# Attention, router and quantized FFN on one core: the out projection's later token tiles by fours with two levels of Strassen-Winograd products, and contexts issued two groups at a time

## The chip, the cores and the metric

The kernel runs on one core of one Trainium2 chip. The metric is the device time of one execution in microseconds (us), median over several runs. TensorE (PE in the profile) multiplies matrices, VectorE (DVE), ScalarE (ACT) and GpSimd (POOL) work element by element, SyncE (SP) issues most of the transfers. Each engine works through its own list of instructions in order; they wait for one another through semaphores.

## The reference, cut to what matters

There are 64 sequences of 64 rows, that is 4096 tokens of 1024 numbers, in float32.

```python
x = x + attn(cond(x))          # cond: einsum('bct,bcd->bdt') with a 64x64 matrix chosen per sequence
                               # attn: qkv = y @ qkvw + qkvb (1024 x 3072); 32 heads of 32; softmax over 64 keys;
                               #       ctx @ attn_ow + attn_ob   (1024 x 1024: "the out projection")
x = x + ffn(cond2(x))          # cond2: x @ W.T + 2 * (top-2 gated low-rank experts)
                               # ffn: int8-like quantized gate, up and down products, silu
```

The change concerns above all `ctx @ attn_ow + attn_ob` and what is added to it, the input x.

## The kernel before, in words

**Tiles.** A token tile is 128 tokens; there are 32, taken as 16 pairs. Attention works on 8 blocks of 4 tiles.

**Strassen-Winograd products.** The large float32 products are not done with 8 products of halves but with 7 (class `Winograd`). The weight matrix is cut into quarters A11 to A22, the tokens' matrix into B11 to B22; sums S1 to S4 of weight quarters and T1 to T4 of token quarters are formed, and `ORDER = (1, 6, 7, 5, 2, 4, 3)` names the seven products, with `A_OF` and `B_OF` their operands. Two products that are to be added share a PSUM bank (`BANK`), so that PE adds the second onto the first: before it may, the engine that has to read the first result alone must have read it. The results are put together by DVE, which adds a PSUM bank to an SBUF tile, and by ACT, which copies.

**Attention** (`attention`). For each block: `conditional` multiplies x by its chosen matrices; `rows_job` makes q and k (each product 4 matmuls of 128x256), `values_job` makes v (8 of 128x256). `run(cost, product, rest)` issues one product on PE and, one product later, its `rest` on DVE and ACT. Beside these run the softmax groups. `group` issues `scores` (two units at once) on PE, then `contexts()`, which issues every waiting group whose transposed probabilities pT are there; softmax, a split of the float32 values into 16-bit planes (`parted`), a DMA transpose (`turned`) and a join (`joined`) follow at planned times, kept in a heap by `at(time, f)`. A group's contexts reach `ctx_d` in DRAM through ACT (`co`). In the first block the weights' sums are made on the chip (`sums`, four operations of DVE or POOL in a row) and stored for the later blocks; in later blocks `chores` halve and combine other weights a piece at a time.

**Out projection** (`OutProjection`). It works by pairs. `pair(p)` gives seven steps of one `product` (4 matmuls of 128x512) and one `rest`. x is loaded from the input and the bias added by POOL (L1140); u1, u2 and u3 are sums of products, added to x by POOL (L1156) or with PSUM by DVE (L1159). `prepare(p + 1)` forms the next pair's T sums on DVE (L1029 to L1032). `turn` splits x into planes and transposes it by DMA, and `turned` joins it and stores it to `xT_d` for the second stage; x itself is stored to the output. Pairs 0 and 1 run inside attention's last phase, beside the last softmax groups; there

```python
length = 24
at(now + 41, contexts)
```

places the last contexts. Pairs 2 to 15 run alone, from `second_stage`, which also loads one 1 MB piece of the next weights W (`loads_t`) per pair.

**Second stage** (`second_stage`). By pairs again: router, seven base products with W, the low-rank part, quantization and the FFN, in an order that is written out by hand. It is not changed but for where its tiles lie and when its weights are loaded.

Matmuls of float32 stand in the records as two instructions each, so a product of 4 matmuls has 8 records.

Of the kernel before, what the change touches and what calls it, by code (L numbers as in the profile page):

```python
# [20 lines left out]
P = 128  # L21
# [15 lines left out]
def adaln_attn_ffn(ctx: ExitStack, tc: tile.TileContext, a, out: bass.AP):  # L37
# [40 lines left out]
    with tc.manual_schedule(), ExitStack() as psum, ExitStack() as early:  # L78
        ps_g = psum.enter_context(tc.tile_pool(name="ps_g", bufs=4, space=PSUM, reuse_waits="tile"))
        st = early.enter_context(tc.tile_pool(name="halve", bufs=2))  # L80
        chores = halve_weights(tc, st, const, dram, srcs, half, any_i)
        chores = itertools.chain(chores, combine_quarters(tc, st, (("wo", a["ow"]), ("wt", a["w_t"])), comb))
        op = OutProjection(tc, a, x_t, out_t, ctx_d, xT_d, ps_g, comb, KC, H)
        attention(tc, a, x_t, ctx_d, ident, dram, ps_g, KC, PB, NBLK, NCH, HPC, H, C, chores, early, op)
        second_stage(tc, a, out_t, xT_d, ident, ps_g, KC, NT, H, C, half, comb, op)

# [96 lines left out]
def attention(tc, a, x_t, ctx_d, ident, dram, ps_g, KC, PB, NBLK, NCH, HPC, H, C, chores, early, op):  # L183
# [27 lines left out]
    with ExitStack() as ctx, ExitStack() as mid:  # L211
# [5 lines left out]
        pTp = pool(ctx, "pT1", 4, side="right")  # L217
        sm = pool(ctx, "sm1", 3, side="right")
        ps_s = pool(ctx, "ps_s", 1, space=PSUM)
# [35 lines left out]

        def held(word, other):


            nc.scalar.copy(word, other[:, 0:1])
# [9 lines left out]
        def sums(eng, at):  # L269
            eng.tensor_tensor(at("S1"), at("A21"), at("A22"), ALU.add)  # L270
            eng.tensor_tensor(at("S2"), at("S1"), at("A11"), ALU.subtract)
            eng.tensor_tensor(at("S3"), at("A11"), at("A21"), ALU.subtract)
            eng.tensor_tensor(at("S4"), at("A12"), at("S2"), ALU.subtract)
# [4 lines left out]
        def load_qk(b, wh, c, eng=None):  # L278
            t = w_qk[b, wh, c] = wp.tile([P, 7, KQ, P], F32, tag="wqk", name=f"w{wh}_{b}_{c}")
            if b == 0:  # L280
# [4 lines left out]
                def rest():  # L285
                    sums(eng or nc.vector, lambda key: t[:, SLOT[key], :, :])
                    nc.gpsimd.dma_start(qk_d[wh, c], t)
                return rest
# [6 lines left out]
        def load_v_raw(g, eng):  # L295
# [9 lines left out]
            def rest():  # L305
                sums(eng, at)
                for slot in range(7):
                    later.append(lambda slot=slot: nc.gpsimd.dma_start(v_d[g][:, slot, :, :], w_v[0, g, slot]))
            return rest

        bqkv = act.tile([P, 3 * KC], F32, tag="bqkv", name="bqkv")
        x_next = load_x(0)
        first_sums = [load_qk(0, "q", 0), load_qk(0, "k", 0, nc.gpsimd)]
        nc.sync.dma_start(bqkv, a["qkvb_t"])
        first_sums.append(load_v_raw(0, nc.gpsimd))
# [62 lines left out]
        def job(name, cost, n, matmuls, put, begin=None, done=None):  # L378
# [4 lines left out]
            def one(i):  # L383
                def product():
                    if i == ORDER[0] and begin:
                        begin()
                    bank = BANK[i]
# [20 lines left out]
            return [one(i) for i in ORDER]  # L408
# [7 lines left out]
        def rows_job(b, c, wh, next_load):  # L416
# [30 lines left out]
            return job(f"ps{wh}{{}}_{b}_{c}", 1.72, HB, matmuls, put, begin, done)  # L447
# [88 lines left out]
        def context(b, c, us, pTs):  # L536
# [11 lines left out]
            for n, u in enumerate(us):  # L548
# [3 lines left out]
                co = p2.tile([P, HB], F32, tag="co", name=f"co_{b}_{c}_{u}")  # L552
                nc.scalar.activation(co, pc[:, n, :], AF.Identity, bias=bqkv[:, 2 * KC + ch:2 * KC + ch + 1])  # L553
                nc.scalar.dma_start(ctx_d[2 * b + t][:, ch, :], co)

# [10 lines left out]
        def contexts():  # L566
            while waiting and len(waiting[0][3]) == 2:
                context(*waiting.pop(0))

        def group(b, c, us):  # L570


            def begin():
                ps = scores(b, c, us)
                contexts()
# [45 lines left out]
        def qk_fill(b, c):  # L621
            fills = []
            for wh in "qk":
                n = qk_jobs.index((b, wh, c))

                def next_load(n=n):
                    if n + 2 < len(qk_jobs):
                        f = load_qk(*qk_jobs[n + 2])
                        if f:
                            pending_sums.append(f)  # L630

                js = rows_job(b, c, wh, next_load)
                if b == 0 and n >= 2:

                    cost, product, rest = js[5]

                    def product_and_sums(product=product):
                        product()
                        if pending_sums:
                            pending_sums.pop(0)()  # L640
                    js[5] = (cost, product_and_sums, rest)
                fills += js
            return fills

        v_raw = []

        def v_fill(b, g):
            def next_load(slot):
                if b == 0 and g + 1 < NV:
                    if slot == SLOT[A_OF[ORDER[-1]]]:  # L650
                        v_raw.append(load_v_raw(g + 1, nc.vector))
# [5 lines left out]
            if (b, g) == (0, 0):  # L657
                cost, product, rest = js[4]

                def product_and_sums():  # L660
                    product()
                    pending_sums.pop(0)()
                js[4] = (cost, product_and_sums, rest)
# [10 lines left out]
        for b in range(NBLK):  # L674
            if b + 1 < NBLK:
                x_next = load_x(b + 1)
            for c in range(NP):
                fills, length = [], None
                if c + 1 < NP:
                    fills += qk_fill(b, c + 1)  # L680
                    if c == 0:
                        fills[7:7] = v_fill(b, 1)
                        if b == 0:
                            cost, product, rest = fills[4]

                            def with_sums(product=product):
                                product()
                                v_raw.pop()()
                            fills[4] = (cost, with_sums, rest)
# [3 lines left out]
                else:  # L693
# [5 lines left out]
                    at(now + 41, contexts)  # L699
# [6 lines left out]
        assert not due and not waiting  # L706
# [350 lines left out]
class OutProjection:  # L1057
# [3 lines left out]
    def __init__(self, tc, a, x_t, out_t, ctx_d, xT_d, ps_g, comb, KC, H):  # L1061
        self.tc, self.a, self.x_t, self.out_t, self.ctx_d, self.ps_g, self.comb = tc, a, x_t, out_t, ctx_d, ps_g, comb
        self.xT_d, self.turning = xT_d, []
        self.KC, self.H = KC, H
        self.NPAIR = len(ctx_d)
        self.stack = ExitStack()
        self.st = {}

    def pool(self, name, bufs):
        return self.stack.enter_context(self.tc.tile_pool(name=name, bufs=bufs, reuse_waits="tile"))  # L1070

    def open_weights(self):

        nc, H = self.tc.nc, self.H
        wp = self.pool("wo3", 1)
        self.cp = [self.pool("co3", 1)]
        ob = self.ob = wp.tile([P, H], F32, tag="ob", name="ob")
        self.A, loads = load_quarters(self.tc, wp, self.comb, "wo", self.a["ow"], self.KC // 2, H // 2)
        return [
            lambda: self.load_ctx(0), loads[0], lambda: nc.sync.dma_start(ob, bcast_rows(self.a["ob"]))  # L1080
        ] + loads[1:]

    def open_rest(self):
        self.cp.append(self.pool("co4", 1))
        self.xp, self.tp, self.up = self.pool("xo3", 2), self.pool("to3", 2), self.pool("uo3", 1)
        self.hp = self.pool("ho3", 2)
# [3 lines left out]
        self.prepare(0)  # L1090

# [5 lines left out]
    def load_x(self, p):  # L1097
        s = self.st.setdefault(p, {})
        s["x"] = self.xp.tile([P, 2, self.H], F32, tag="x", name=f"xo_{p}")
        for t in range(2):  # L1100
            self.tc.nc.sync.dma_start(s["x"][:, t, :], self.x_t[2 * p + t])

    def prepare(self, p):
        s, KQ = self.st[p], self.KC // 2
# [4 lines left out]
    def turn(self, p, t):  # L1109

        nc, n = self.tc.nc, self.H // 2
        for f in range(2):
            h = self.hp.tile([P, 2, n], I16, tag="h", name=f"xh_{p}_{t}_{f}")
            nc.scalar.copy(h, planes(self.st[p]["x"][:, t, f * n:(f + 1) * n]))  # L1114
            hT = self.hp.tile([P, 2, n], I16, tag="hT", name=f"xhT_{p}_{t}_{f}")
            nc.sync.dma_start(
                hT.rearrange("p h (k q) -> p (h k) q", q=P), h.rearrange("p h n -> p (h n)"), transpose=True
            )
# [556 lines left out]
```

## Time and profile before

| what | value |
|---|---|
| median of 3 runs | 2479.53 us (2477.33 to 2479.58) |
| the profiled execution's own time | 2482.55 us |
| its span, first to last instruction | 2480.8 us |
| granted TensorE clock, mean | 0.992 |
| attention, up to the first out projection product | 0 to 1386.6 us |
| out projection, pairs 0 to 15 | 1386.6 to 1784.0 us |
| second stage | 1784.0 to 2480.8 us |
| busy in the out projection alone (1456 to 1788): PE, DVE, ACT, POOL | 332.0, 113.5, 131.9, 120.6 of 332 us |
| DMA there | 0.78 of 16 engines, 241 GB/s |

The page gives busy time by engine, the span in 40 slices, the chain of work that ended last, and the costliest groups of instructions. A row such as `L1159 DVE TENSOR_TENSOR xo<-pod,xo 128x512 ... x29 | 20.0, 690 | 62.6 <-PE pod` says: line 1159, on DVE, 29 times, 20.0 us in all, 690 ns each, and 62.6 us in which DVE stood idle ahead of them, ended by PE. A busy PE is modelled at the ends of its matmuls, so the distance between starts is what one costs.

### The profile page before, as it was taken

The page shows a single profiled execution, that of the slowest core. Times are in us where ns is not written, and L with a number is a line of the kernel's source. Part 1 is how long each engine was busy: PE and PEld are TensorE (multiplying, and loading weights), DVE is VectorE, ACT ScalarE, POOL GpSimd, SP SyncE. Part 2 cuts the span into 40 slices and gives each one's busy share as a digit, 9 for nine tenths or more (in the row PEclk, how much of TensorE's full clock was granted, in tenths as well). Part 3 has the DMA queues.
Part 4 walks back from the last instruction along what each step waited for, and adds up shares of the span by engine and source line. Part 5 has one row for each costly group of instructions (what it writes and reads, how often), then busy time and mean ns, then how long its engine had stood idle before and what let it go on. Part 6 is the DMA issues. An engine that isn't in the chain of part 4 may idle for free.

```text
span 2480.8 us, 34182 instructions
## 1 busy us (share of the span) xinstructions
PE 2435.7 (98%) x13232; PEld 1703.8 (69%) x13232; DVE 1524.9 (61%) x2957; ACT 953.6 (38%) x1303; POOL 360.8 (15%) x451
## 2 busy tenths in 40 slices
PE   8999999999999999999999999999999999999996
PEld 7888888888888888888888644444454545454452
DVE  4585585675764755745646623333367777778787
ACT  1243353443443533533534533343423333333333
POOL 5010011011122221110000233334200000000001
PEclk9999999999999999999999999999999999999997
DMA  8795767676677667766646668877744443434343
GB/s 281 262 266 153 225 192 232 191 208 203 205 201 246 206 188 248 201 202 181 171 145 215 187 213 248 271 232 239 227 151 79 87 79 81 85 73 91 71 96 70
DMA packets 417980, 446.76 MB, mean 180 GB/s; under 512 B 299665, under 2 KB 353938, under 8 KB 404114
## 3 DMA queue, kind: packets, MB, share of 16 engines
q1 hardware_dynamic: 387298, 377.90, 52.5%
q0 software_dynamic: 12080, 49.82, 7.6%
q10 hardware_dynamic: 18432, 16.79, 2.0%
q8 instruction: 106, 1.74, 0.3%
q14 instruction: 64, 0.52, 0.1%
HBM read 272.97 MB, written 100.66 MB: 151 GB/s over the span
## 4 chain that ended last, share of the span: by engine, by line
PE 95%; DVE 3%; DMA 1%; issue 1%; ACT 0%; SPq 0%; ACTq 0%; DVEq 0%
PE pska L428 5%; PE psva L455 5%; PE poc L1019 5%; PE pskc L428 4%; PE psvc L455 4%; PE pskd L428 4%; PE psqd L428 4%; PE pbc L1019 4%; PE pba L1019 4%; PE psvd L455 4%; PE psqa L428 4%; PE poa L1019 4%; PE pod L1019 4%; PE pbd L1019 4%; PE psqc L428 4%; PE s L491 3%
## 5 line engine op out<-in xcount | busy, mean ns | idle before, releaser
L533 ACT COPY pT<-phT 128x1024 int16<-128x1024 int16 x128 | 167.2, 1342 | 84.8 <-DMA phT<-ph 84.6
L553 ACT ACTIVATE co<-c,bqkv 128x256 f32<-128x256 f32 x128 | 60.6, 473 | 295.2 <-PE c L543 253.6
L503 DVE TENSOR_REDUCE mx<-s 128x8 f32<-128x512 f32 x128 | 88.3, 690 | 138.0 <-PE s L491 128.4
L521 ACT COPY ph<-prob 128x1024 int16<-128x1024 int16 x128 | 131.4, 1046 | 43.4 <-DVE prob L515 42.7
L414 DVE SCALAR_TENSOR_TENSOR kbd<-pskd,bqkv,psku 32x256 f32<-32x256 f32 x256 | 122.6, 479 | 30.9 <-PE pskd L428 27.2
L507 ACT ACTIVATE prob<-prob 128x512 f32<-128x512 f32 x128 | 78.9, 628 | 154.4 <-DVE prob L504 130.6
L1140 POOL TENSOR_TENSOR xo<-xo,ob 128x1024 f32<-128x1024 f32 x32 | 82.5, 2597 | 375.7 <-DMA xo<-in_x_dram 371.2
L428 PE MATMUL psqa<-yB,wq 128*128 128x256 f32 x512 | 123.5, 384 | 0.0
L428 PE MATMUL pska<-yB,wk 128*128 128x256 f32 x512 | 122.6, 382 | 0.0
L1483 POOL DMA_DIRECT2D out_dram<-y x29 | 25.2, 869 | 653.4 <-DVE y L1475 653.4
L1114 ACT COPY xh<-xo 128x1024 int16<-128x1024 int16 x64 | 64.1, 1040 | 143.8 <-DVE xo L1159 143.4
L455 PE MATMUL psva<-wv,yB 128*128 128x256 f32 x512 | 117.7, 383 | 0.0
L1019 PE MATMUL poa<-woA,cx 128*128 128x512 f32 x256 | 115.3, 593 | 0.0
L1019 PE MATMUL pba<-wtA,x1T 128*128 128x512 f32 x256 | 115.1, 592 | 0.0
L1125 ACT COPY xTo<-xhT 128x1024 int16<-128x1024 int16 x64 | 84.8, 1341 | 64.1 <-DMA xhT<-xh 62.3
L455 PEld LDWEIGHTS psva<-wv,yB 128*128 128x128 f32 x512 | 96.8, 191 | 13.4
L428 PEld LDWEIGHTS pska<-yB,wk 128*128 128x128 f32 x512 | 96.0, 190 | 14.3 <-issue 1.4
L428 PEld LDWEIGHTS psqa<-yB,wq 128*128 128x128 f32 x512 | 95.2, 190 | 13.7 <-issue 0.2
L513 DVE TENSOR_REDUCE den<-prob 128x8 f32<-128x512 f32 x128 | 86.8, 678 | 17.4 <-ACT prob L507 17.2
L504 DVE TENSOR_TENSOR prob<-s,mx 128x512 f32<-128x512 f32 x128 | 88.6, 692 | 9.7 <-DVE mx L503 0.9
L515 DVE TENSOR_TENSOR prob<-prob,den 128x512 f32<-128x512 f32 x128 | 89.8, 702 | 4.4
L412 ACT ACTIVATE kbd<-pska,bqkv 32x256 f32<-32x256 f32 x128 | 59.6, 466 | 79.2 <-PE pska L428 77.6
(243 smaller groups left out, 5138.5 us busy)
## 6 DMA issues: line engine op xcount, KB each, us to landing
wv<-v_d SPq DMA_DIRECT2D x98, 512.0 KB, 3.8
wq<-q_d SPq DMA_DIRECT2D x28, 1792.0 KB, 8.1
wk<-k_d SPq DMA_DIRECT2D x28, 1792.0 KB, 8.2
x<-in_x_dram SPq DMA_DIRECT2D x32, 512.0 KB, 9.8
ctx_d<-co ACTq DMA_DIRECT2D x128, 128.0 KB, 5.6
cx<-ctx_d SPq DMA_DIRECT2D x16, 1024.0 KB, 7.0
xo<-in_x_dram SPq DMA_DIRECT2D x32, 512.0 KB, 5.7
xT_d<-xTo SPq DMA_DIRECT2D x64, 256.0 KB, 4.1
```

The source lines that it names most:

```text
L414: nc.vector.scalar_tensor_tensor(dst, ps, bias, u, ALU.add, ALU.add)
L428: nc.tensor.matmul(ps[:, 0:HB], A[:, SLOT[A_OF[i]], k, :], B[B_OF[i]][:, k, :], start=first and k == 0, stop=k == KQ - 1, skip_group_check ...
L455: nc.tensor.matmul(ps[:, j * VC:(j + 1) * VC], B[B_OF[i]][:, k, j * P:(j + 1) * P], A[:, k, :], start=first and j == 0 and k == 0, stop=k ...
L503: nc.vector.tensor_reduce(mx_v, ps, AX.X, ALU.max)
L504: nc.vector.tensor_tensor(p.rearrange("p (a e) k -> p a e k", a=2), ps, mx_v.unsqueeze(3).to_broadcast([P, 2, HPC, C]), ALU.subtract)
L513: nc.vector.tensor_reduce(den, p, AX.X, ALU.add)
L515: nc.vector.tensor_tensor(p, p, den.unsqueeze(2).to_broadcast([P, n, C]), ALU.mult)
L521: nc.scalar.copy(h, planes(p.rearrange("p n k -> p (n k)")))
L533: nc.scalar.copy(planes(pT.rearrange("p a b q -> p (a b q)")), hT)
L1019: self.nc.tensor.matmul(ps, self.B[self.B_OF[i]][:, k, :], self.A[self.A_OF[i]][:, k, :], start=first and k == 0, stop=k == self.KQ - 1, s ...
L1125: nc.scalar.copy(planes(xT.rearrange("p k q -> p (k q)")), hT)
L1140: nc.gpsimd.tensor_add(s["x"][:, t, :], s["x"][:, t, :], self.ob)
```

## The change

Pairs 0 to 3 stay as they were. The other 24 token tiles are taken in six quads of four. A quad is one outer Strassen-Winograd product over 512 tokens; each of its seven products (256 tokens by 512 by 512) is again made of seven inner products of 2 matmuls of 128x256, except product 1 of the first quad, which stays plain. The outer products run in sets (1 and 6, 5 and 3, 7 and 4, then 2 alone; in the last quad 7 and 2, then 4), two side by side in PSUM pools `ps_g` and `ps_h`. The inner weight sums are made once, on DVE, during pairs 2 and 3 (`next_sums`); the outer and inner token sums on DVE in each quad, partly for the next quad, one set on POOL. x is taken in four quarters; results of shared sums are added to them by POOL (`add`).

Further edits come with it. In attention, x + bias is formed by POOL while x lies on the chip and stored to the output (`residual`), from where the out projection loads it; the next block's x is loaded later. The contexts are issued only when two groups are ready, with more buffers, and their copies are spread in time. The first block's weight sums are issued one or two to a product instead of four in a row, and its first q job takes product 2 second. The weights of the second stage go into the room of the inner sums, four of seven pieces during the last quad and three after it; small constants of the second stage are made earlier; its tiles lie in the room of the out projection's weights (`room`).

```diff
@@ attention
+        def residual(i, xt):
+            nc.gpsimd.tensor_add(xt, xt, ob)
+            nc.gpsimd.dma_start(out_t[i], xt)
...
-        def contexts():
-            while waiting and len(waiting[0][3]) == 2:
-                context(*waiting.pop(0))
+        def contexts(least=1):
+            ready = sum(len(pTs) == 2 for *_, pTs in waiting)
+            for n in range(ready if ready >= least else 0):
+                context(*waiting.pop(0), 1.7 * n * (least - 1))
...
                 ps = scores(b, c, us)
-                contexts()
+                if behind:
+                    behind.pop()()
+                contexts(2)
...
+                js = rows_job(b, c, wh, next_load, (1, 2, 6, 7, 5, 4, 3) if n == 0 else ORDER)
...
+                    for at_, count in ((5, 2), (6, 2)):
+                        with_sums(js, at_, pending_sums, count)
...
-                            fills[4] = (cost, with_sums, rest)
+                            for at_ in range(3, 7):
+                                with_sums(fills, at_, v_raw, 1)
...
-                    at(now + 41, contexts)
+                    at(now + 20, contexts)
...
-        assert not due and not waiting
+        assert not due
+        contexts()
+        assert not waiting
@@ class OutProjection
+    PAIRS = 4
+    SETS = ((1, 6), (5, 3), (7, 4), (2,))
+    LAST = ((1, 6), (5, 3), (7, 2), (4,))
...
+    def outer_sum(self, p, *keys):
...
+            self.tc.nc.vector.tensor_tensor(T, ops[x], ops[y], ALU.subtract)
...
+    def inner_sums(self, p, i, eng, which=range(4)):
...
+            eng.tensor_tensor(B[key], B[x], B[y], ALU.subtract)
...
+    def quad(self, p, used):
...
+        def add(q, v):
+            nc.gpsimd.tensor_tensor(self.x[q], self.x[q], v, ALU.add)
...
+            for k in range(2):
+                nc.tensor.matmul(
+                    ps, B[:, k, :], A[:, k, :], start=first and k == 0, stop=k == 1, skip_group_check=True
+                )
...
+        def rest(i, j, ps, v):
...
+            m, t, w = {5: (1, 1, 7), 2: (0, 0, None), 4: (1, 0, 6), 3: (0, 1, 6)}[j]
...
+            old = part(res[{6: 1, 7: 6}[i]], m, t) if i in (6, 7) else dst
+            nc.vector.tensor_tensor(dst, ps, old, ALU.add)
+            if w is not None:
+                nc.gpsimd.tensor_tensor(dst, dst, v[w], ALU.add)
...
+        extra = {
+            (0, 2): [lambda: self.outer_sum(p, "T3")], (0, 3): [lambda: self.outer_sum(p, "T4")],
+            (0, 4): [sums(sets[1][1], nc.gpsimd)], (0, 5): [sums(sets[1][0])],
+            (1, 4): [sums(sets[2][0])], (1, 5): [sums(sets[2][1])],
+            (2, 4): [sums(sets[3][0], which=range(3))], (3, 1): [sums(sets[3][0], which=(3,))],
+        }
...
+            extra[0, 1] = [sums(1, which=(3,)), sums(6, which=(3,))]
+        if not last:
+            extra[2, 2] = [lambda: self.outer_sum(p + 2, "T1", "T2")]
+            extra[2, 5] = [lambda: self.inner_sums(p + 2, 1, nc.vector, range(3))]
+            extra[3, 3] = [lambda: self.inner_sums(p + 2, 6, nc.vector, range(3))]
...
+            for s, j in enumerate(Winograd.ORDER):
...
+                for i, ps in zip(idx, out):
+                    rest(i, j, ps, vs[i])
+                for f in extra.get((n, s), ()):
+                    f()
...
+            elif n == 1:
+                self.load_raw(p + 2, "B22")
+                add((0, 0), res[1])
+                add((0, 1), res[5])
+                add((1, 1), res[5])
+                finished((0, 1), 7)
...
+            elif n == 2:
+                add((1, 0), res[7])
+                add((1, 1), res[7])
@@ second_stage
+        used = [lambda: load_wt(0), lambda: load_wt(1), lambda: load_x1(0), lambda: load_wt(2), lambda: load_wt(3)]
+        for p in range(op.PAIRS, NPAIR, 2):
+            op.quad(p, used)
+        op.close()
...
+        for n in (4, 5, 6):
+            load_wt(n)
```

The numbers in `extra` are (set, step of the set): after the `rest` of that step the named sums are issued.

## The prediction

> **What bounds the kernel now.** I began with the page: busy shares, the 40 slices, the chain that ended last.
>
> ```profile
> PE 2435.7 (98%) x13232; PEld 1703.8 (69%) x13232; DVE 1524.9 (61%) x2957; ACT 953.6 (38%) x1303; POOL 360.8 (15%) x451
> ...
> PE 95%; DVE 3%; DMA 1%; issue 1%; ACT 0%; SPq 0%; ACTq 0%; DVEq 0%
> ```
>
> TensorE is busy throughout, and the chain runs through it for 95% of the span. Time is won only by giving PE less to do, or by closing its idle gaps. The gaps are in PE's list of waits (us in total, times, longest):
>
> ```profile
> PE c L543 <- ACT pT L533: 5.9, 1, 5.9
> PE psqd L428 <- DVE qT L414: 3.0, 1, 3.0
> PE psqb L428 <- DVE wq L271: 1.6, 1, 1.6
> ```
>
> There is none in the out projection. Its products stand in PE's timeline like this (start, us, what):
>
> ```profile
> 1495.61 3.60 PE L1019 MATMUL poa<-woA,cx 128*128 128x512 f32 x8
> 1499.04 3.60 PE L1019 MATMUL pob<-woS,To 128*128 128x512 f32 x8
> ```
>
> Not the length counts (ends are modelled) but the step from start to start: a product of 8 records costs 3.433 us, and a pair of token tiles 7 products, 24.03 us. In attention the 256-wide products start every 1.73 us for 8 records (psqa 69.19 and after), that is 0.216 us a record against 0.429 for a 512-wide one, though the weight loads then fill PEld (190 ns of each 216). So halving the width halves the price.
>
> Then I looked at what the two vector engines do there, by shape:
>
> ```profile
> L1032 DVE TENSOR_TENSOR To<-cx,To 128x512 f32<-128x512 f32 x13 | 26.1, 2008 | 0.0
> L1030 DVE TENSOR_TENSOR To<-cx,To 128x512 f32<-128x512 f32 x13 | 9.0, 692 | 0.4
> L1140 POOL TENSOR_TENSOR xo<-xo,ob 128x1024 f32<-128x1024 f32 x26 | 67.1, 2601 | 56.4 <-DMA xo<-in_x_dram 51.8 <-issue 4.5
> ```
>
> The same operation on the same shape takes 692 ns in one place and 2008 ns in another. The timelines of POOL and DVE say why:
>
> ```profile
> 1463.72 5.10 POOL L1140 TENSOR_TENSOR xo<-xo,ob 128x1024 f32<-128x1024 f32 x2 [1.14 <-DMA xo<-in_x_dram]
> ```
> ```profile
> 1463.78 2.84 DVE L1031 TENSOR_TENSOR To<-cx 128x512 f32<-128x512 f32 x1
> 1466.54 2.83 DVE L1032 TENSOR_TENSOR To<-cx,To 128x512 f32<-128x512 f32 x1
> ```
>
> Each DVE sum of two SBUF tiles waits out one whole POOL add (2.45 us), then runs in 0.6. The adds with one PSUM input (L1159, 0.69) are not held, even beside POOL. Today this costs nothing: PE needs those sums much later.
>
> [...] after the idle 5.94 us at 1438 one product takes 5.21 us instead of 3.43, and after 3.03 us at 83 the next two take 2.68 and 4.29 instead of 1.73 and 3.45. I price it at 1.8 us per idle of 3 us or more[...].
>
> **The change part by part.** The sum is made against the profiled execution: 2482.6 us, span 2480.8. The median is 2479.5, 3.1 less.
>
> *Quads.* Twelve pairs become six quads, each of four sets of outer products: 1 and 6, 5 and 3, 7 and 4, then 2 alone. Before: 12 x 24.03 = 288.4. After: a quad is 7 outer products of 7 inner products of 4 records of 256 columns, 7 x 7 x 4 x 0.216 = 42.3; in the first one product stays plain (16 records of 0.429 = 6.9 instead of 6.0). 6 x 42.3 + 0.8 = 254.5. **-33.9 us**, on PE, hence on the path.
>
> *DVE and POOL in a quad.* From the issue order: 40 adds out of PSUM (128x256, 0.42 by L402), 24 inner sums (0.42), 4 outer sums (128x1024, 1.22 by L371): 32 us of 42.3, against 34% busy now. POOL: 6 adds of 1024 (2.45) and 19 operations of 256 (no row; between 0.455 for 128 and 1.24 for 512, I take 0.7): 28 us. Both fit alone, but [...] DVE is in order, so what waits behind a held sum are the PSUM adds that give PE its banks back. I walked one steady quad by hand, PE's step being 1.73 us:
> - After the second set (24.2 us into the quad) POOL gets three 2.45 us adds, from 26.9 on. The next quad's T1 and T2 come at 29.8 on DVE; T1 waits for the second add (31.8) and ends at 33.0, T2 waits for the third (35.2) and ends at 36.4. Queued behind them is the PSUM add of inner product 5, which frees the bank of inner product 3; PE wants that at 34.5 and gets it at 36.7: it waits **2.2**.
> - DVE stays behind: the same bank of the set's last step comes free at 42.5, wanted at 41.1: **1.4**.
> - POOL then has two more 2.45 us adds, and three inner sums of the next quad stand ahead of the PSUM add that frees bank "a", with which the next quad begins: **4.6**, or **2.4** if DVE had not been behind; at 4.6 the clock adds **1.8**.
>
> The full price is 10 us a quad; the low end is 0 to 1, if DVE wins its ties (a wait cannot be a gain). I take 4.6 (2.2 and 2.4) for five quads, since the delays partly cover each other, and 2 for the last, which prepares no successor: **+25** (2 to 52).
>
> *Start.* The first q job takes product 2 second: its operands need no weight sums. The wait of 1.6 goes, but the quarter B21 is copied only at about 20.0: -1.2. Sums of v weights are spread one to a product instead of four in a row ahead of qT: the 3.0 goes with its slow clock: -4.8. **-6.0** (0 to -7). The bias row now loaded ahead of the v weights delays POOL's sums by some 2 us; they were done at 39 and wanted from 47: nothing.
>
> *End of attention.* The last contexts move behind one more product, which covers 3.43 of the 5.94 us. What remains, 2.5[...]: **-5.2** (0 to -7.7); late next is the same pT, behind SP's stores.
>
> *Contexts by two groups.* PE issues the same 128 context products in 4 bursts a block instead of 7. A burst alone starts at 1.08 us for 32 records, and 48 together take 1.5, so a burst saved is worth 0.07: 8 x 3 x 0.07 = **-1.7** (+1 to -3). The copies out of them wait longer, with two more pT buffers; PE needs nothing from them.
>
> *Residual.* x + bias moves from the out projection to attention: 32 POOL adds of 2.45 and 32 stores of 512 KB from POOL's queue (0.87 each to issue, row L1483), together 106 us of POOL, which is 15% busy there; the loads in the out projection stay, by quarters. Each add may hold a DVE sum 2.45 us, ahead of PSUM adds with slack. The x loads of the next block move some 25 to 50 us later, still ahead of their use by one phase. **+1** (0 to +4). SP's queue: same number of x loads; 16.8 MB more DMA over 1380 us is 12 GB/s on 210.
>
> *Weight sums* for the quads: 28 DVE sums of 0.69 in pairs 2 and 3, two per 3.43 us: covered, since POOL has lost its 2.6 us adds there.
>
> *Second stage's weights.* They came one per pair, long before; now four in the last quad, three after all turns in SP's queue. ACT needs 4 x 1.04 + 4 x 1.34 = 9.5 us for those turns, so the fifth is issued some 11 us past the quad's end and lands (9.5 us, row wtA) at about 20; PE wants it at 19.2 (1803.25 against 1784.0). **+2** (0 to 10).
>
> Sum: -33.9 + 25 - 6.0 - 5.2 - 1.7 + 1 + 2 = -18.8: 2463.8 profiled, **2460.7** as a median.
>
> **The rivals.**
> 1. *The cover holds*: DVE's sums slip between POOL's adds and a quad loses 1 us at most. For it: L1153 and L1159 have idle time ahead of them everywhere (62.6 us ahead of pod), and PE has four more banks (ps_h). Against: the 2008 ns. -33.9 + 7 - 12.9 + 1 = -38.8: 2440.7.
> 2. *DVE becomes the bound, and the kernel is slower*: the walk in full, at the turn between quads. 52 instead of 25: +8.2 on the profile, 2487.7; with the second stage's weights at +6 it is 2492. It decides from 8.4 us a quad on: the other terms come to -41.8, the last quad's 2 included, and there are five such quads.
> 3. *DMA*: a quad moves what two pairs did, 10.1 MB, in 42.3 us instead of 48. The share was 0.76 (234 GB/s, 1600 to 1790, wt loads included); it rises to about 0.8, and in the last quad, with 5 MB of weights and x, over 0.85. That makes raw B22 land late (issued at 24.2, wanted at 33), or the second stage start late: +8 on my sum, 2469. Small, as landings of 1 MB stand at 7 us.
>
> **How the numbers follow.** A measurement of this kernel tells about 0.2%, 5 us, from no change. Mine 0.40 (0.33 faster, 0.05 same, 0.02 slower), cover holds 0.34 (all faster), DVE-bound 0.18 (0.04 same, 0.14 slower), DMA 0.08 (0.06 faster, 0.01 and 0.01). Faster 0.73, same 0.10, slower 0.17. Low end: rival 1 with start, tail, residual and contexts at their best, 2435, and half of what it leaves in the quads gone too, 2432. High end: rival 2, 2492. I name 2460.
>
> **What would show it.** Right: quads of 46 to 48 us, PE waiting in them for DVE (names q<-iT or q<-xq, u), DVE's 128x256 SBUF sums at a mean well over 0.42 us, and the out projection some 10 us shorter. The waits for qT at 83 and for wq at 21 gone; the wait for pT at 1438 under 3 us. Wrong: quads at 42 to 43 with sums at 0.42 (rival 1), over 50 (rival 2), or PE waiting on rB, xq or wt from DMA (rival 3).

## The result and the profile after

The changed kernel takes 2492.7 us (median of 6 runs, 2491.1 to 2495.8) against 2479.6 for the kernel before on the same chip: ratio 1.0058, 95% interval 1.0047 to 1.0069. It is slower. The profiled execution has a span of 2490.1 us, 9.3 more than before.

The page of the changed kernel: the busy line, and the chain that ended last.

```profile
PE 2410.9 (97%) x13686; PEld 1798.4 (72%) x13724; DVE 1683.3 (68%) x3264; ACT 966.4 (39%) x1345; POOL 512.2 (21%) x597
...
PE 25%; DMA 1%; DVE 1%; ACT 1%; issue 1%; SPq 0%; ACTq 0%; DVEq 0%
```

PE has 25 us less to do, and the span is longer: the gaps have grown. PE's share of the chain is a quarter of the span instead of 95%. Followed back from the end, the chain stays mostly on PE to the start of the second stage; there it passes to the transfers of the last quad's turned copies, and it begins only at 1770 us. Some of its pieces in order of time (start, us, what):

```profile
1777.82 3.60 DMA xT_d<-xTo
1781.42 5.33 DMA xhT<-xh
1788.24 6.23 DMA xT_d<-xTo
1807.02 6.45 DMA wtA<-in_w_t_dram
1813.52 5.41 PE pba L1043 x8
```

PE's waits, of which these are the ones that matter here (us in total, times, longest):

```profile
PE qd L1334 <- DVE u L1371: 12.0, 10, 1.9
PE qb L1334 <- DVE xq L1371: 10.6, 5, 2.1
...
PE ghp L1647 <- DVE gh L1634: 6.2, 1, 6.2
PE psvb L470 <- DVE T L384: 5.1, 2, 2.6
PE qa L1334 <- ACT v L1357: 5.0, 3, 2.3
```

The waits for pT, qT and wq of before are gone. New are waits in the quads (qa to qd), at the start of the second stage (ghp), and two in attention for the token sums T that the products of v need (psvb). In the quads, DVE's sums by shape (1540 to 1740 us):

```profile
L1282 DVE TENSOR_TENSOR iT<-T12q,iT 128x256 f32<-128x256 f32 x17 | 20.6, 1210 | 0.3
L1282 DVE TENSOR_TENSOR iT<-T12q 128x256 f32<-128x256 f32 x17 | 17.9, 1052 | 0.0
...
L1272 DVE TENSOR_TENSOR T12q<-rB,T12q 128x1024 f32<-128x1024 f32 x4 | 12.3, 3064 | 0.9 <-DMA rB<-ctx_d 0.9
L1272 DVE TENSOR_TENSOR T4q<-rB,T12q 128x1024 f32<-128x1024 f32 x4 | 4.9, 1216 | 0.0
```

T4 shows the free time of an outer sum, 1.216 us; T2 of the next quad (the first of the two rows), the same operation, takes 3.064. Inner sums, 0.42 us where nothing holds them, take over 1 us in the mean. These are the sums that stand beside POOL's wide additions; the row of before where a T sum took 2008 ns has lost its neighbour on POOL (L1140) and runs free:

```profile
L1320 POOL TENSOR_TENSOR xq<-xq,u 128x1024 f32<-128x1024 f32 x17 | 41.0, 2421 | 0.6
```
```profile
L1054 DVE TENSOR_TENSOR To<-cx,To 128x512 f32<-128x512 f32 x4 | 2.8, 692 | 0.1
```

Where it hurts is seen in a table by stretch, for one steady quad (us, then busy time of PE, PEld, DVE, ACT, POOL, with instruction counts, PE's clock, DMA share, GB/s):

```profile
1543.00:1573.00 30.00, 29.69 (x130) 25.86 (x131) 19.66 (x45) 13.79 (x16) 15.23 (x15) 0.94 1.00 265
1573.00:1593.00 20.00, 15.37 (x68) 12.24 (x66) 19.36 (x26) 7.74 (x10) 15.31 (x11) 1.00 0.51 129
```

In the first 30 us DVE is busy two thirds of the time and PE always. In the last 20 us (the third and fourth set and the turn to the next quad) DVE is busy 97% and PE loses 4.6 us. The DMA share falls to 0.51 there, and no wait of PE in the quads is for a transfer. The end of that stretch on DVE, and on PE the first product of the next quad that waits for it:

```profile
1587.43 1.90 DVE L1282 TENSOR_TENSOR iT<-T12q 128x256 f32<-128x256 f32 x1
1589.36 2.47 DVE L1282 TENSOR_TENSOR iT<-T12q,iT 128x256 f32<-128x256 f32 x1
1591.75 0.94 DVE L1282 TENSOR_TENSOR iT<-T12q 128x256 f32<-128x256 f32 x1
1592.62 0.41 DVE L1371 TENSOR_TENSOR xq<-qa,xq 128x256 f32<-128x256 f32 x1
```
```profile
1589.92 1.03 PE L1334 MATMUL qa<-woS,T12q 128*128 128x256 f32 x4
1593.08 1.99 PE L1334 MATMUL qb<-s,iT 128*128 128x256 f32 x8 [2.13 <-DVE xq L1371]
```

Three inner sums for a product that PE needs later stand ahead of the addition out of PSUM (xq<-qa) that gives PE its bank back. They take 5.2 us, where 1.7 (0.42, 0.84 and 0.42) are their free times.

By the starts of PE's instructions the 9.3 us are made up like this:

| stretch | before | changed | difference |
|---|---|---|---|
| up to the out projection's first product | 1386.6 | 1387.0 | +0.4 |
| from there to the first quad (pair 4 before) | 109.0 | 101.0 | -8.1 |
| six quads (twelve pairs) | 288.4 | 298.4 | +10.0 |
| second stage's first pair, router to router | 32.1 | 41.8 | +9.7 |
| the rest | | | -2.7 |

### The profile page after: what moved, and what is told of

It is laid out like the page before. It is cut to its first block, busy times and chain, and to the rows that moved or that the text cites. A ratio compares the mean times of both kernels' runs of the same rounds, so it can differ in the third digit from the quotient of the medians.

```text
span 2490.1 us, 35994 instructions
## 1 busy us (share of the span) xinstructions
PE 2410.9 (97%) x13686; PEld 1798.4 (72%) x13724; DVE 1683.3 (68%) x3264; ACT 966.4 (39%) x1345; POOL 512.2 (21%) x597
## 5 line engine op out<-in xcount | busy, mean ns | idle before, releaser
L260 POOL TENSOR_TENSOR x<-x,ob 128x1024 f32<-128x1024 f32 x32 | 76.7, 2398 | 150.5 <-PE cond L363 128.6
L485 DVE TENSOR_TENSOR vbd<-psvd,psvu 64x256 f32<-64x256 f32 x128 | 54.0, 422 | 55.2 <-PE psvd L470 53.7
L429 DVE SCALAR_TENSOR_TENSOR kbd<-pskc,bqkv,psku 32x256 f32<-32x256 f32 x128 | 61.5, 481 | 40.3 <-PE pskc L443 38.6
```

Of the source, the lines that this page charges most:

```text
L429: nc.vector.scalar_tensor_tensor(dst, ps, bias, u, ALU.add, ALU.add)
```

## Experiments

Each run also has a ratio to the kernel before on the same chip; ratios are compared, since the kernel before took medians of 2478.0 to 2481.1 us on the four chips of these runs. "Quads" and "first pair" are the third and fourth row of the table above, each read from the run's one trace. Four traces in which the quads' code is the same (the changed kernel and the three runs on the start of the second stage) give 297.8 to 298.6 us for the quads, so a difference of 1 us there means little.

### The wide additions in the quads

**Left out.** The body of `add` is empty, so six additions of 128x1024 a quad are missing.

```diff
-            nc.gpsimd.tensor_tensor(self.x[q], self.x[q], v, ALU.add)
```

> The changed kernel without the 128x1024 additions on GpSimd (six a quad), so the quarters of the outer products' combinations aren't added up; all else is issued as before. If GpSimd's wide additions hold VectorE (its outer sums at 2.3 to 3.1 us instead of 1.2, the next quad's inner sums at 1.1 to 1.9 instead of 0.42), the quads fall from 49.8 us each to 43 to 45, the waits of TensorE for xq and u go, and the kernel is 27 to 36 us faster than the changed one: 2457 to 2466. If VectorE's own work, the DMA queues or the clock sets the quad's length, the quads stay at 48 us or more: 2482 to 2493.

2474.1 us, ratio 0.9967 (0.9954 to 0.9979), quads 274.5 us, the first pair 45.1. That is less than was expected. The wait for xq is gone, and the next quad's outer sums are free; the wait for u is halved (6.3 us). Outer sums of this run:

```profile
L1272 DVE TENSOR_TENSOR T12q<-rB,rB 128x1024 f32<-128x1024 f32 x4 | 4.9, 1226 | 5.6 <-DMA rB<-ctx_d 5.6
L1272 DVE TENSOR_TENSOR T12q<-rB,T12q 128x1024 f32<-128x1024 f32 x4 | 4.9, 1225 | 4.0 <-DMA rB<-ctx_d 4.0
```

With the additions go the long sums, and the quads are 24 us shorter. DVE now even waits for the raw quarters (1.0 to 1.4 us each time), so there is slack. The second stage gives 3 us of it back. But the quads are still 20 us longer than the 254.5 that their products need: 13 us are waits of PE for ACT's v and DVE's u. So the wide additions are not all that the prediction had left out; and this run doesn't tell whether they cost by their hold of DVE or by what waits for their results.

**On DVE, at the same places.**

```diff
-            nc.gpsimd.tensor_tensor(self.x[q], self.x[q], v, ALU.add)
+            nc.vector.tensor_tensor(self.x[q], self.x[q], v, ALU.add)
```

> The changed kernel with its 128x1024 additions (six a quad) on VectorE instead of GpSimd, at the same places of the order. If the time lost in the quads is VectorE's waiting for GpSimd's wide additions and not VectorE's own work, then 6 x 1.22 = 7.3 us of new VectorE work per quad replaces about 11 us of stretched sums, none of it at one place: the quads take 274 (as without the additions) to 285 us instead of 298, and the kernel 2470 to 2480. If VectorE's amount of work is the bound, 7.3 us more of it a quad make the quads longer than 298 us: 2493 to 2530.

2492.1 us, ratio 1.0060 (1.0047 to 1.0073), quads 298.1 us. Neither side of the expectation: the outer sums were free (1.22 us), so it was POOL's additions that held them, and yet nothing was gained. DVE's timeline of this run shows a new wait:

```profile
1582.95 2.36 DVE L1320 TENSOR_TENSOR xq<-xq,u 128x1024 f32<-128x1024 f32 x2 [1.19 <-POOL xq L1373]
1585.23 0.42 DVE L1359 TENSOR_TENSOR v<-qb,v 128x256 f32<-128x256 f32 x1
```

The wide additions wait for POOL's last narrow one on the same x, and then keep the read of PSUM behind them (v) from starting; PE waits for v 2.9 us in nearly every quad (14.7 us in 5 waits).

**On DVE, those in a row spread** over the next set's steps (the second and third due 1.7 and 3.4 us later):

```diff
+                self.at(delay, lambda: nc.vector.tensor_tensor(x, x, v, ALU.add))
```

> As the run before, but where two or three wide additions follow one another, the later ones come 1.7 and 3.4 us of planned time later, between the steps of the next set. If three in a row (3.7 us) hold VectorE's reads of PSUM long enough for TensorE to wait, this takes up to 2 us a quad off: 2460 to 2478. If not, it equals the run before.

2492.5 us, ratio 1.0056 (1.0043 to 1.0068), quads 294.5 us. The first of the two additions of product 7 still stood at the set's start; the wait for v stayed (15.6 us in 6 waits).

**On DVE, those of product 7 later too** (1.7 and 3.4 us into the fourth set). The order of the two late ones after the second set is also exchanged.

```diff
-                add((1, 0), res[7])
-                add((1, 1), res[7])
+                add((1, 1), res[7], 1.7)
+                add((1, 0), res[7], 3.4)
```

> The changed kernel with the wide additions on VectorE, as in the two runs before, but those on (1,1) and (1,0) of the product 7 due 1.7 and 3.4 us into the next set instead of at its start, where VectorE stood 1.19 us waiting for GpSimd's last 128x256 addition and then ran two wide ones (2.36 us) ahead of a read of PSUM that TensorE waited 2.9 us for in every quad. If the lost gain of those runs is that one wait at the turn of the quad, the six quads take 274 to 282 us instead of 298: 2469 to 2477. If VectorE's amount of work holds them, the wait turns up elsewhere and the quads stay at 48 us and more: 2488 to 2494.

2496.2 us (2489.9 to 2502.2), ratio 1.0076 (1.0063 to 1.0090), quads 296.9 us. My first theory, that this one wait had eaten the gain, falls here. It fell from 2.9 to 1.2 us, and others came or grew: for iT (10.3 us in 6 waits) and for ACT's v (8.2 in 7). The traced execution, 2489.9, is the fastest of the five. DVE in this run, ahead of and within the end of a quad:

```profile
1539.00:1569.00 30.00, 26.49 (x122) 22.74 (x121) 20.98 (x40) 13.54 (x16) 8.34 (x10) 1.00 0.98 259
1569.00:1585.00 16.00, 13.73 (x62) 11.17 (x61) 15.36 (x30) 5.37 (x6) 5.21 (x7) 1.00 0.48 154
```

In the second stretch DVE is 96% busy, and no wide addition of POOL stands beside it: DVE's own work (6 x 1.22 = 7.3 us more a quad) fills what the hold had filled. Either DVE's amount of work in a quad is the bound, or only that stretch is. The next three runs tell these apart.

**Two of the six left out**, those that fall into the stretch.

```diff
-                add((1, 0), res[7])
-                add((1, 1), res[7])
```

> The changed kernel without the two wide GpSimd additions of product 7 at the end of each quad's third set; the other four remain. If the end of the quad is the bound, these two are worth most of what all six were: the six inner sums beside them (1.90, 2.47 and 0.94 us where 0.42, 0.84 and 0.42 are their free times) fall by 3.6 us, TensorE's wait for xq (2.1 us with the slow products behind it) goes, and the quads take 280 to 285 us instead of 298 (all six left out: 274.5): 2475 to 2480. If every addition costs alike, a third of 24 us: 290 us, 2485.

2481.8 us, ratio 1.0011 (1.0005 to 1.0018), quads 285.4 us, at the edge of what was expected. A third of the additions is worth 13.0 of the 24 us: what they cost depends on where they stand. The wait for xq is gone.

**Three inner sums a set earlier**, the amount unchanged. For the room of the third buffer, the row bm is loaded only when the second stage starts (its lines are not shown).

```diff
-self.pool("iq3", 2)
+self.pool("iq3", 3)
...
-            (2, 4): [sums(sets[3][0], which=range(3))],
+            (1, 3): [sums(sets[3][0], which=range(3))],
```

> The changed kernel with three of VectorE's inner sums (those of product 2: 1.9 us) done in the second set of a quad instead of the third, for which the pool of inner sums gets a third buffer; the row bm, whose memory it takes, is loaded when the second stage starts. VectorE's amount of work is the same. If the bound is the end of each quad, where VectorE is busy 97% for 20 us, the quads are shorter by up to 1.9 us each: 287 to 290 us for six instead of 298, the kernel 2482 to 2485. If the amount is the bound, or GpSimd's hold simply moves, the quads stay at 296 to 299: 2491 to 2493.

2487.7 us, ratio 1.0029 (1.0018 to 1.0040), quads 291.5 us: -6.9 from moving 1.9 us of sums a quad, a little less than the 8 to 11 that were expected.

**The same with the wide additions on DVE and later.**

> The wide additions on VectorE and later (its quads took 296.9 us, VectorE busy without a pause for 16 us at the end of each), with the same three sums a set earlier. If the place is what counts, 1.9 us a quad go: 286 to 289 us for six, about 10 us less than that run. If the amount counts, 295 to 298.

2485.6 us, ratio 1.0030 (1.0021 to 1.0040), quads 287.4 us, 9.5 less than without the move. So the place counts: with the same amount of work, what DVE has to do at the end of each quad costs more than elsewhere. Not shown is that this is all. At 287.4 the quads equal the twelve pairs of before (288.4), and no more; 33 us over the 254.5 remain, of which 26.1 are waits of PE, the longest for iT (1.6 to 2.5 us, some 16 us into a quad).

### The start of the second stage

In the changed kernel PE waits 6.2 us for the gated rows gh. ACT's timeline tells why (start, us; in brackets the idle time before, and what ended it):

```profile
1801.09 2.53 ACT L1161 COPY xTo<-xhT 128x1024 int16<-128x1024 int16 x2 [1.60 <-DMA xhT<-xh]
1805.25 1.33 ACT L1161 COPY xTo<-xhT 128x1024 int16<-128x1024 int16 x1 [1.63 <-DMA xhT<-xh]
1806.45 0.57 ACT L1676 COPY bp<-pba 128x512 f32<-128x512 f32 x1
1807.03 1.28 ACT L1625 ACT_TABLE_LOAD   x1
1808.32 0.20 ACT L1625 ACTIVATE g<-d 128x2 f32<-128x2 f32 x1
```

The router's d was ready at 1792.8 on DVE, but its sigmoid stands behind the last quad's turning copies, each of which waits for a transpose.

**Leftover copies on POOL.** `turn` and `turned` copy with `self.copy`, which is ACT's until `close`.

```diff
     def close(self):
+        self.copy = self.tc.nc.gpsimd.tensor_copy
         self.run_due(math.inf)
```

> The changed kernel with the turning copies that are left when the last quad ends (the halves of x and their turned halves, 128x1024 of 16 bits) on GpSimd instead of ScalarE. If the second stage's first gates wait because the router's sigmoids stand behind these copies in ScalarE's queue (d ready at 1792.8, sigmoid at 1808.3), TensorE's wait of 6.2 us for gh goes, with the slow product behind it: 6 to 8 us less than the changed kernel, 2485 to 2487. If the second stage's later start is a matter of its weights' transfers, it stays at 2492.7.

2491.5 us, ratio 1.0038 (1.0024 to 1.0051), first pair 44.1 us. The wait for gh went, and this came:

```profile
PE pba L1043 <- DMA wtA<-in_w_t_dram: 8.6, 1, 8.6
```

The weights' last three pieces are requested behind the copies' transfers in SP's queue, and POOL's copies put these off. In all, this run can't be told from the changed kernel.

**Weights requested first.**

```diff
+        for n in (4, 5, 6):
+            load_wt(n)
         op.close()
...
-        for n in (4, 5, 6):
-            load_wt(n)
```

> The changed kernel with the leftover turning copies on GpSimd, and the second stage's last three weight tiles requested ahead of those copies' transfers in SyncE's queue. With the copies alone moved, TensorE waited 8.6 us for wtA in place of 6.2 us for gh: two late things, one behind the other. If these two are all, the first pair of the second stage (from its router to the next one's) takes 32 to 34 us as in the kernel before instead of 41.8: 2483 to 2486 in all. If the transfers are late by the DMA queues' load, it stays at 2489 to 2492.

2489.6 us, ratio 1.0049 (1.0036 to 1.0062), first pair 40.8 us. A third thing was behind the second:

```profile
PE pbd L1043 <- DVE z L1686: 6.5, 1, 6.5
```

DVE stood 18.8 us ahead of z, until the transfer xT_d<-xTo of the last copy: z lies in the memory that the turning tiles give back.

**z laid elsewhere**, with the two edits before it kept (a tile y of the same pool is laid out ahead of z).

> The run with the weights' requests ahead of the leftover copies, and the tiles z of the second stage moved in SBUF (another tile of their pool is laid out first), away from the memory that the leftover copies still use; there z stood 18.8 us until the last of their transfers, and TensorE 6.5 us behind it. If gates, weights and memory are the three things that the late end of the last quad's copies holds, the first pair of the second stage now takes 32 to 35 us (before 32.1, changed 41.8): 2481 to 2485. If a fourth is behind them (the rows inv_gate came 3 us late for VectorE), it stays above 2487.

2485.9 us, ratio 1.0035 (1.0021 to 1.0048), first pair 34.7 us instead of 41.8. The late copies held an engine's queue, a DMA queue and a piece of memory; freeing one or two showed the next, and only all three gave the time back. A fourth is behind them: what is left over the 32.1 us of before is a wait of PE of 2.5 us for the second pair's x1T, which is read from these copies' transfers.

### Attention

**Attention's edits alone**, all sixteen pairs and the second stage as before.

> The kernel before with the change's attention alone (contexts by two groups with four to six tiles behind them, sums of the weights spread, first job's order, bias added to x on GpSimd in attention), and all sixteen pairs of the out projection and the second stage as before. If the reading of the changed kernel's trace is right (its quads begin 7.6 us earlier than the pair that stands there before), this gives 2479.6 - 7.6 = 2472, with the two waits of TensorE for the condition's sums T (2.65 and 2.42 us) in it. If the prediction's sum for attention held (-6.0, -5.2, -1.7, +1), it gives 2467.7. If the attention part loses, it is above 2480.

2476.2 us, ratio 0.9976 (0.9967 to 0.9986): a gain of 3.5 to 8.2 us. 2472 is at the interval's edge. The two waits for T are in it. Its second stage isn't quite as before: the first pair takes 36.0 us instead of 32.1, and 35.8 and 35.7 in the next two runs. There the router's first sum lg starts 0.3 us after the last turned copy's transfer lands, in all three traces. In the changed kernel it starts 0.3 us after its product, so this is no part of that kernel's loss. The likely reason is memory, as with z, but no run tested it.

**The bias 16 us later.**

```diff
-                        at(now + 8 * j + 4, lambda i=b * PB + j, xt=xt: residual(i, xt))
+                        at(now + 8 * j + 20, lambda i=b * PB + j, xt=xt: residual(i, xt))
```

> As the run with attention alone, but the four GpSimd additions of the bias in each block are due 16 us later (from 20 us into the block's first chunk instead of 4). If they hold VectorE's sum T of 128x1024 (3.86 us where it takes 1.22 beside nothing), both waits of TensorE for T go, and the slow products behind them (5.41 instead of 3.62): some 8 us less than with attention alone, near 2464. If T is late because the contexts or other VectorE work come earlier in its queue, nothing changes: 2472.

2475.6 us, ratio 0.9977 (0.9969 to 0.9986). The expectation failed. One of the two waits went, the one at 194 us: there the additions now stand behind a cast on POOL that waits for its operand until 258 us. The one at 1226 us stayed. POOL and DVE there, in this run:

```profile
1218.58 2.62 POOL L259 TENSOR_TENSOR x<-x,ob 128x1024 f32<-128x1024 f32 x1 [128.46 <-PE cond L362]
```
```profile
1221.67 3.87 DVE L383 TENSOR_TENSOR T<-yB,T 128x1024 f32<-128x1024 f32 x1
```

POOL had been idle for 128 us and ran the addition as soon as PE had read x. A due time sets only the place in an engine's order; where nothing stands ahead, as here, it delays nothing.

**In the last block the bias on DVE**, which has other work ahead of it there; the additions of the other blocks are due later, as in the run before.

```diff
-            nc.gpsimd.tensor_add(xt, xt, ob)
+            (nc.vector if i >= NBLK * PB - PB else nc.gpsimd).tensor_add(xt, xt, ob)
```

> The run with attention alone and the bias later, and in the last block the four additions of the bias on VectorE, whose queue is never empty, so that their place in the order delays them (GpSimd's queue was empty, and ran them as soon as x was free). If that was what held T, the remaining wait of TensorE (2.42 us, with a slow product of 5.41 instead of 3.62) goes: about 4 us less, 2471. If VectorE's four additions of 1.2 us make scores or products wait instead, it stays at 2475.

2467.0 us, ratio 0.9950 (0.9937 to 0.9963). Both waits for T are gone, and the last block takes 170.5 us up to the out projection, where it took 174.9 with attention's edits alone and 175.1 in the run before. This is what the edit explains; in the traces the blocks ahead of it, whose code is the same as in the run before, are 5.9 us shorter as well.

**Contexts alone** on the kernel before.

> The kernel before with the contexts by two groups alone (six tiles pT, four tiles co, the copies of the second group 1.7 us later, the last contexts 20 us into the last chunk and at the end). By the trace of before it takes away one wait of TensorE for pT (5.94 us) with the slow stretch behind it (5.38 instead of 3.60): about -7.7, near 2472. If the pairing itself helps each chunk (a shorter context in slow succession), it gains more: to 2468. If the last contexts only wait for something else (copies co), nothing: 2479.

2466.5 us, ratio 0.9949 (0.9936 to 0.9963): more than the one wait. By the starts of cond the third to sixth block take 170.3 to 170.7 us instead of 171.3 to 172.1, about 1 us less each (the second took 2.6 us more, the seventh 3.5 less), and the stretch from the first out projection product to the second stage is 7.9 us shorter.

**Attention without the moved bias.**

> The change's attention alone, but the bias added in the out projection as before, so that GpSimd adds nothing to x in attention. Contexts alone gave -12 us (2466.5 against 2478.3); the edits of the first block (sums of the weights spread, the first job's order) took 3.4 us off it in the traces. If both stand, this gives 2463. If the first block's edits give back what they take (psqc and psva wait for VectorE's sums later), 2466 to 2467; if the lower gain of the whole attention part was not the bias, 2472 and more.

2461.8 us, ratio 0.9935 (0.9922 to 0.9948). The interval lies wholly below that of attention with the bias on POOL (0.9967 to 0.9986): the moved bias costs about 0.4%, 10 us. The two traced executions are 17 us apart: 8.9 in the two blocks with the waits for T, 3.9 in the second stage's first pair (lg, above), the rest mostly in small pieces in attention. This version beats both kernels, and so do contexts alone.

### All mendings together

> All mendings together: the wide additions on VectorE and later, the bias on VectorE in the last block and later, leftover copies on GpSimd, weights requested first, z moved. If the pieces add up: quads -18 to -24, the two waits for T with their slow products -9, the second stage's start -8, from 2492.7: 2452 to 2458, which would be below the kernel before and below attention alone with its bias mended (2467.0). If the quads don't gain, 2473 to 2477.

2481.5 us, ratio 1.0010 (1.0003 to 1.0016), hardly above the kernel before, and above the 2473 to 2477 expected if the quads didn't gain. In the trace, an execution of 2477.9 us, attention and the second stage gained as in their own runs (first pair 34.9 us); the quads did not (298.4): their wide additions were on DVE and later, the form whose quads took 296.9 us, without the sums a set earlier.

## Why the prediction was wrong

It named 2460 and a faster kernel. The waits that it feared in the quads came where it had put them, but the term that prices them was too small, and so were two others.

- **Arithmetic of the quads, -33.9: right.** Away from the waits a product of 4 records steps 0.86 us, and a steady quad's 196 records are 42.3 us. (6 x 42.3 + 0.8 is 254.6, not 254.5; nothing hangs on it.)
- **DVE and POOL in a quad, +25: the term that failed; the quads lost 43.9** (298.4 - 254.5). It counted the idle time of three waits in a steady quad, and nothing for the clock, for what surrounds a wait, or for the first quad's own start. In the trace the 43.9 us are 29.8 of idle time in 21 waits, 6.8 in four spells of half clock, and 7.3 that stands mostly around the waits, some 0.35 for each. By quads, counted from one wait for xq to the next:
  - Steady quads take 48.1 to 49.8 us, 6.9 over 42.3 in the mean. In the quad from 1543 to 1593 the waits are 1.51 and 0.96 us for u and 2.13 for xq, 4.6 together, and 4.6 was the value taken. That is luck: the prediction had taken 2.2 and 2.4, for the first and the last, and left the middle one out as covered. What surrounds the waits came on top, and in some quads the clock: the price was for idles of 3 us or more, but after the 2.12 us of idle at 1543 two products of 8 records step 3.01 and 2.24 us instead of 1.73, and single idles of 1.85 to 2.12 us were enough three times in the quads. The last section lists these idles, and those that were as long and kept full clock.
  - The first quad lost 10.5 us: PE also waited 2.3 us there for ACT's copy v, which stood behind the turning copies of the last pair.
  - The last quad, for which I took 2, lost 5.7 with two waits for ACT's and DVE's v.
- **The rival that came true** is the second, DVE as the bound: DVE is 90 to 97% busy in the 20 us ahead of each wait for xq, and the runs that take work away there gain. Its threshold, 8.4 us in five quads and 2 in the last, is 44 us; the six lost 43.9, the steady ones less and the first and the last more. That alone would have made the two kernels equal. The change is slower because the next two terms failed as well. (Rival 1's sum leaves out the +2 of the second stage; with it, it is 2442.7.)
- **Residual, +1: measured about +10** (0.9976 against 0.9935), of which up to 3.9 (lg) isn't in the changed kernel. I had written that a held DVE sum stands ahead of additions with slack. But in two blocks POOL had nothing else and came at once, and the held sum was T, which PE wants next: two waits of 2.65 and 2.42 us, each with a product of 5.41 us behind it instead of 3.62.
- **Second stage, +2: measured +7.0.** The weights were late, as I said, and later: the fifth piece landed some 27 us after the quad's end, not 20. Not foreseen were the router's sigmoids in ACT's queue behind the same copies, and z in their memory.
- **Start, -6.0**: the first block took 169.6 us without the moved bias, 174.5 before, so -4.9, of which contexts alone gave 1.2. **End and contexts, -6.9**: contexts alone gave about 12 us, as PE's wait for pT went wholly and four of the blocks gained about 1 us each, where I had 0.2 (a burst saved at 0.07 us). Without the bias this part gave 16 us, more than the 12.9 of the sum; with it, the changed kernel gained 7.7 us up to the first quad, where start, end, contexts and residual add up to 11.9.

Of what I had named as signs: the steady quads went over 46 to 48 us and stayed just under the 50 of rival 2; PE waited for DVE's u and xq; there was no wait for DMA in the quads (rival 3); the out projection was not 10 us shorter but 2 us longer.

What stays open: why blocks gain 1 us from contexts by two; what part of the 24 us of the wide additions is their hold of DVE; and whether the 33 us that remain in the best form of the quads can be had.

## What to carry to other kernels

Busy shares over a stage hide where an in-order engine has no slack: look at it in stretches of a few microseconds around the turn of the loop, and judge each added operation by the stretch it falls into, not by the engine's mean. When a loop ends, ask what its leftovers still hold: the queue of an engine, a DMA queue, a piece of memory; here little was gained until all three were free. A planned time delays an operation only on an engine that is busy until then (POOL, idle for 128 us, ran its addition at once). And a trace of each part alone (contexts, attention without the bias) would have shown that the best of this change lay outside the quads.

## What was not expected of the hardware

- PE's clock halved after idles shorter than 3 us, but not after every idle of that length. In the trace of the changed kernel PE has twelve waits of 1.5 us or more in the quads. Half clock (0.50, for 3.41 us each time) came with those of 2.12 us at 1543, 1.85 at 1677, 2.04 at 1690, and 2.14 at 1780.5 with another of 1.24 at 1782.9. The clock stayed full with 2.32 us at 1501, with 2.13 at 1593, 1641 and 1740, and with four of 1.5. So it isn't the length of an idle alone; what else decides was not shown. The stretches around the idle at 1543 and the one at 1593 (busy time of PE, PEld, DVE, ACT, POOL, then PE's clock):

```profile
1540.52:1543.93 3.41, 1.28 (x7) 0.81 (x6) 3.40 (x5) 2.24 (x4) 2.38 (x3) 1.00 0.60 145
1543.93:1547.35 3.42, 3.42 (x10) 2.71 (x9) 1.11 (x4) 1.56 (x3) 1.15 (x2) 0.50 1.05 254
1588.30:1591.72 3.42, 2.65 (x13) 1.99 (x11) 3.39 (x2) 2.15 (x4) 3.42 (x3) 1.00 0.14 33
1591.72:1595.13 3.41, 2.05 (x10) 1.82 (x11) 2.39 (x6) 2.75 (x3) 2.11 (x3) 1.00 0.88 193
```

- A wait of PE in the quads of the changed kernel cost more than its idle time even at full clock: the step to the waiting product is 0.16 us longer than the free step and the idle together (the idle is counted from the modelled end of the matmul before), and that product takes 0.97 us instead of 0.86. At 1593 the step is 3.16 us, with 2.13 of idle.
- A DVE sum of 128x1024 beside a POOL addition of the same width took up to 3.87 us (T in attention at 1222; T2 in the quads 3.06 in the mean) instead of 1.22, and of the short ones beside the additions at 1587 two took 1.90 and 2.47 us instead of 0.42.
